# Keys and values per chunk and half of the heads, the next graph projected over four groups, tails without a lock, statistics two rows per step, longer gaps after residual transfers, denominators one step later

## The chip, the cores and the metric

The kernel runs on one NeuronCore of one Trainium2 chip. The metric is the device time of that core in microseconds (us). Every time below is a median of several executions. Each ratio compares a kernel with the kernel before, run on the same chip in the same rounds.

## The reference

One graph transformer layer over 8 graphs of 2048 nodes and 256 channels in fp32, all with one adjacency matrix. There are 8 heads of 32 channels.

```python
qkv = x @ w_qkv                                   # split in q, k, v, 8 heads of 32
scores = q @ k^T / sqrt(32), -1e9 where adj == 0
t = softmax(scores) @ v
x1 = layernorm(x + t) ;  f = relu(x1 @ w1 + b1) @ w2 + b2
out = layernorm(x + layernorm(x1 + f))            # x: the layer's input
```

## The kernel before

The work is a list of 1024 **items**: graph `f`, chunk of 512 queries `qc` (0 to 3), half of the heads `g` (0, 1) and block of 128 keys `mb` (0 to 15). Sixteen items with the same `f, qc, g` are a **group**. A step of the loop issues the scores of item t+2 and the values of item t, and slips in one or two **fillers**: pieces of projections, of denominators, of the tail of a chunk (attention output, norms, feed-forward, output). An **eviction** is the DVE instruction that adds the mask to scores in PSUM and writes them to a buffer p; two make one item, and ACT then takes the exp in place. A p buffer comes free when its values matmuls are done and its sum, on POOL or by a **chained add** (a transfer that accumulates one p into another), has been taken. A **residual** is the transfer that adds the layer's input x to a tail's rows; **statistics** are the means and variances of a norm. A **lump** is a step in which the loop must finish several projection banks at once.

```python
pp = tile_pool(name="pp", bufs=9)     # p: exp of the scores, 128 x 2048 fp32, 1 MB
ap = tile_pool(name="ap", bufs=1)     # acc: ONE accumulator of the same size
POOLED = (0, 1, 4, 7, 9, 12, 14)      # items whose p is summed on POOL into acc
CHAINS = ((2, 5, 8, 11), (3, 6, 10, 13))   # items summed by accumulating DMA
SUM = 4

def add_up(item):
    f, qc, g, mb = item
    grp = (f, qc, g)
    for chain in CHAINS:
        if mb in chain[1:]:           # "chained add"
            nc.gpsimd.dma_start(PT[f, qc, g, chain[0]], PT.pop(item), accum_op=ALU.add)
    if mb == POOLED[1]:
        ACC[grp] = ap.tile([P, 4, CH], F32, name="acc")
        nc.gpsimd.tensor_tensor(ACC[grp], PT.pop((f, qc, g, POOLED[0])), PT.pop(item), ALU.add)
    elif mb in POOLED[2:]:
        nc.gpsimd.tensor_tensor(ACC[grp], ACC[grp], PT.pop(item), ALU.add)

def denominator(f, qc, g):            # started SUM steps after the group's last item
    terms = [PT.pop((f, qc, g, LAST))] + [PT.pop((f, qc, g, chain[0])) for chain in CHAINS] + [ACC.pop(grp)]
    ps = bank()                       # while items run, there is ONE spare PSUM bank
    # ... 32 matmuls of ones with the terms into ps, a copy dT by ACT
    yield 1
    # ... 4 transposes of dT into bank(), read by DVE: rc = 1 / den
    if g == 1: start(items.index((f, qc, g, LAST)) + SUM + 2, tail(f, qc), urgent=True)

def norm(t):                          # three times per tail
    for j in range(TPC):              # TPC = 4 rows
        nc.vector.bn_stats(st, t[:, j, :]); nc.vector.bn_aggr(mv[:, j, :], st)
    yield 1                           # ... then POOL and ACT scale the rows

def tail(f, qc):
    while state["y"]: yield 0         # the lock: one tail at a time
    state["y"] = True
    # ... y = attention output / denominator (PE transposes, DVE)
    nc.gpsimd.dma_start(y, xin, accum_op=ALU.add)      # residual
    yield 4
    yield from norm(y)
    # ... feed-forward in fillers yT, w1, w2; second norm
    nc.gpsimd.dma_start(z, xin, accum_op=ALU.add)      # second residual
    yield 5
    yield from norm(z)
    nc.sync.dma_start(out[...], z)
    state["y"] = False

# in the loop, step t:
if mb:
    advance(t)                        # one filler
    if mb % 2: advance(t)             # in odd steps a second one
scores(items[t + LEAD]); values(items[t]); add_up(items[t])
```

PE's order is the program's order.

## Time and profile before

| kernel before | |
|---|---|
| time, median of 4 runs | 4099.34 us (4098.45 to 4102.65) |
| busy: PE, DVE, ACT, POOL | 81%, 67%, 60%, 64% |
| p buffers | 9, of 1 MB each |

The prediction below shows the main rows of the profile. A list of waits gives engine, tile and line, what it waited for: us in total, times, longest. The first view is the list of waits (engine, tile and line, what it waited for: us in total, times, longest), the second the page's rows for the first feed-forward matmuls and for the transfers of p (count, size, median us from issue to landing).

```profile
POOL acc L215 <- PE x L248: 147.0, 12, 16.7
...
DVE rc L259 <- PE x L254: 69.0, 8, 9.3
...
DVE p L181 <- DMA p<-p: 19.2, 9, 4.4
```

```profile
L300 PE MATMUL x<-turned,w1s 128*128 128x512 f32 x256 | 128.8, 626 | 3.3 <-ACT turned L292 1.0
...
p<-p POOLq DMA_DIRECT2D x384, 1024.0 KB, 9.3
```

By the list, POOL's first sum of a group waits for the old denominator 12 times of 64; the evictions on DVE hardly ever wait for a chained add to give back a p buffer (19 us), and the w1 matmuls find their PSUM bank free (3.3 us idle). The first of these is misleading: a wait for several things is put down to the one that came last by the profile. Set beside the denominators in the trace, the first sum starts within 0.4 us after their last matmul in all 63 groups that have an old denominator, both tiles that it adds having long been ready.

A measure is worked out from the trace: PE's **idle stretches** of over 0.3 us between the first and the last scores, summed by what the instruction that ended them waited for. For "behind an eviction", the wait is followed one step further, to what held DVE.

### The profile page before, as it was taken

The page shows a single profiled execution, that of the slowest core. Times are in us where ns is not written, and L with a number is a line of the kernel's source. Part 1 is how long each engine was busy: PE and PEld are TensorE (multiplying, and loading weights), DVE is VectorE, ACT ScalarE, POOL GpSimd, SP SyncE. Part 2 cuts the span into 40 slices and gives each one's busy share as a digit, 9 for nine tenths or more (in the row PEclk, how much of TensorE's full clock was granted, in tenths as well). Part 3 has the DMA queues.
Part 4 walks back from the last instruction along what each step waited for, and adds up shares of the span by engine and source line. Part 5 has one row for each costly group of instructions (what it writes and reads, how often), then busy time and mean ns, then how long its engine had stood idle before and what let it go on. Part 6 is the DMA issues. An engine that isn't in the chain of part 4 may idle for free. (4 is left out here: it accounts for less than half of the span.)

```text
span 4091.3 us, 52692 instructions
## 1 busy us (share of the span) xinstructions
PE 3308.0 (81%) x21508; PEld 1011.5 (25%) x21508; DVE 2745.5 (67%) x3175; ACT 2443.2 (60%) x1953; POOL 2624.4 (64%) x1355
## 2 busy tenths in 40 slices
PE   7777788878887888888878878877888878888883
PEld 3222132212222222222222222222222222222221
DVE  3777756777567774777647776477755777567772
ACT  4565555666566664666647666466655666556662
POOL 1576655776567774777747776477754777557774
PEclk9899899999999999999999999999999999999996
DMA  4766745666556664567746667376654677546663
GB/s 122 160 139 150 175 97 105 137 134 147 109 108 144 144 138 99 109 134 152 153 94 130 127 132 150 83 150 145 131 115 99 136 148 157 110 101 135 134 130 74
DMA packets 138792, 525.52 MB, mean 128 GB/s; under 512 B 10160, under 2 KB 76848, under 8 KB 85296
## 3 DMA queue, kind: packets, MB, share of 16 engines
q0 software_dynamic: 89088, 436.24, 53.4%
q1 hardware_dynamic: 49456, 85.86, 6.6%
q8 instruction: 170, 2.79, 0.3%
q14 instruction: 78, 0.64, 0.0%
HBM read 98.44 MB, written 20.97 MB: 29 GB/s over the span
## 5 line engine op out<-in xcount | busy, mean ns | idle before, releaser
L181 DVE TENSOR_TENSOR p<-s,mask 128x1024 f32<-128x1024 f32 x2048 | 2410.5, 1219 | 968.3 <-PE s L178 827.2
L183 ACT ACTIVATE p<-p 128x2048 f32<-128x2048 f32 x1024 | 1951.4, 1910 | 1326.1 <-DVE p L181 1135.6
L217 POOL TENSOR_TENSOR acc<-acc,p 128x2048 f32<-128x2048 f32 x320 | 1505.2, 4704 | 201.5 <-ACT p L183 196.8
L178 PE MATMUL s<-qT,kT 32*128 32x512 f32 x8192 | 1230.3, 671 | 472.9 <-DVE p L181 472.9
L195 PE MATMUL x<-p,v 128*32 128x512 f32 x8192 | 1140.1, 630 | 28.7 <-ACT p L183 28.4
L215 POOL TENSOR_TENSOR acc<-p 128x2048 f32<-128x2048 f32 x64 | 290.9, 4546 | 655.0 <-ACT p L183 508.0
L178 PEld LDWEIGHTS s<-qT,kT 32*128 32x128 f32 x8192 | 333.8, 191 | 1175.7 <-DVE p L181 1077.8
L212 POOL DMA_DIRECT2D p<-p x384 | 362.9, 977 | 362.9 <-ACT p L183 166.3
L195 PEld LDWEIGHTS x<-p,v 128*32 128x32 f32 x8192 | 163.9, 110 | 857.3 <-issue 480.1
L146 PE MATMUL x<-turned,wqkv 128*128 128x512 f32 x480 | 249.2, 645 | 50.9 <-ACT kT L148 29.0
L224 DVE BATCH_NORM_STATS2 st<-y 128x6 f32<-128x256 f32 x384 | 153.9, 401 | 144.3 <-DMA y<-in_x_dram 144.3
L235 ACT ACTIVATE y<-y,nb,rs 128x256 f32<-128x256 f32 x384 | 198.3, 588 | 62.1 <-POOL nb L232 62.1
L248 PE MATMUL x<-p,ones 128*32 128x512 f32 x1536 | 183.1, 610 | 15.8 <-ACT qT L148 14.8
L146 PEld LDWEIGHTS x<-turned,wqkv 128*128 128x128 f32 x480 | 85.4, 197 | 221.1 <-issue 79.8
L158 PE MATMUL x<-wqkv,turned 128*128 128x256 f32 x448 | 112.9, 395 | 31.1 <-ACT v L160 10.1
L300 PE MATMUL x<-turned,w1s 128*128 128x512 f32 x256 | 128.8, 626 | 3.3 <-ACT turned L292 1.0
L309 PE MATMUL x<-w2s,hT 128*128 128x256 f32 x512 | 127.6, 392 | 3.9 <-ACT hT L301 1.3
L228 POOL TENSOR_SCALAR rs<-mv 128x4 f32<-128x4 f32 x96 | 18.4, 191 | 147.9 <-DVE mv L225 144.2
L309 PEld LDWEIGHTS x<-w2s,hT 128*128 128x128 f32 x512 | 92.0, 189 | 69.1 <-ACT hT L301 31.1
L229 POOL TENSOR_TENSOR rs<-rs,mhalf 128x4 f32<-128x4 f32 x96 | 99.5, 1036 | 8.0
L158 PEld LDWEIGHTS x<-wqkv,turned 128*128 128x128 f32 x448 | 81.6, 192 | 77.3 <-ACT qT L148 28.5
L291 PE MATMUL x<-ident,y 128*128 128x128 f32 x256 | 44.6, 294 | 66.9 <-ACT turned L292 46.4
(70 smaller groups left out, 1550.0 us busy)
## 6 DMA issues: line engine op xcount, KB each, us to landing
p<-p POOLq DMA_DIRECT2D x384, 1024.0 KB, 9.3
y<-in_x_dram POOLq DMA_DIRECT2D x64, 512.0 KB, 7.2
mask<-md SPq DMA_DIRECT2D x28, 1024.0 KB, 15.4
in<-in_x_dram SPq DMA_DIRECT2D x32, 512.0 KB, 21.7
in<-in_adj_dram SPq DMA_DIRECT2D x32, 512.0 KB, 5.9
out_dram<-y SPq DMA_DIRECT2D x32, 512.0 KB, 8.3
md<-mask SPq DMA_DIRECT2D x4, 1024.0 KB, 12.7
wqkv<-in_L_gnn_w_qkv_dram SPq DMA_DIRECT2D x1, 768.0 KB, 4.6
```

Source lines behind the costliest of these rows:

```text
L146: nc.tensor.matmul(ps, wqkv[:, a, k0 + g * P:k0 + (g + 1) * P], xT[:, a, :], start=(a == 0), stop=(a == 1))
L158: nc.tensor.matmul(ps[:, (j - jj) * C:(j - jj + 1) * C], xT[:, a, j * P:(j + 1) * P], wqkv[:, a, 2 * C:], start=(a == 0), stop=(a == 1))
L178: nc.tensor.matmul(ps2[half][:, j, :], KT[f, mb // TPC][r:r + D, g, (mb % TPC) * P:(mb % TPC + 1) * P], QT[f, qc][r:r + D, g, :], start=Tr ...
L181: nc.vector.tensor_tensor(pt[:, 2 * half:2 * half + 2, :], ps, MK[f, qc][:, mb, None, :].to_broadcast([P, 2, CH]), ALU.add)
L183: nc.scalar.activation(pt, pt, AF.Exp, scale=1.0 / math.sqrt(D))
L195: nc.tensor.matmul(O[grp][r:r + D, :], V[f, mb // TPC][:, mb % TPC, g * P + r:g * P + r + D], PT[item][:, h, :], start=(mb == 0), stop=(mb ...
L212: nc.gpsimd.dma_start(PT[f, qc, g, chain[0]], PT.pop(item), accum_op=ALU.add)
L215: nc.gpsimd.tensor_tensor(ACC[grp], PT.pop((f, qc, g, POOLED[0])), PT.pop(item), ALU.add)
L217: nc.gpsimd.tensor_tensor(ACC[grp], ACC[grp], PT.pop(item), ALU.add)
L235: nc.scalar.activation(t[:, j, :], t[:, j, :], AF.Identity, bias=nb[:, j:j + 1], scale=rs[:, j:j + 1])
L248: nc.tensor.matmul(ps[r:r + D, :], cst["ones"], term[:, h, :], start=(n == 0), stop=(n == 3))
L309: nc.tensor.matmul(ps[:, (j - jj) * C:(j - jj + 1) * C], hT[:, d, j * P:(j + 1) * P], w2s[:, d, :], start=(d == 0), stop=(d == 1))
```

## The change

Intent: free K and V buffers half by half, so that the next graph's projections can be spread over four groups instead of running in lumps; let tails overlap, so that residual transfers no longer stand beside output and mask transfers; halve the DVE work that statistics put in one step. The denominators come one step later.

```diff
-    kp = ... bufs=NCK + 1          # and vp
+    kp = ... bufs=2 * NCK + 2      # tiles of half the heads; and vp
     # project(f, c): K and V written per half g; V by 16 matmuls of 128 columns per half
-            store[f, c] = dst
+                    KT[f, c, g] = pool.tile([P, CH], F32, name=name)
+        for g in range(2):
+            V[f, c, g] = vp.tile([P, TPC, P], F32, name="v")
-    SUM = 4
+    SUM = 5
     # norm
-        yield 1
+            if j % 2:
+                yield 1
     # tail
-        while state["y"]:
-            yield 0
-        state["y"] = True
         nc.gpsimd.dma_start(y, xin, accum_op=ALU.add)
-        yield 4
+        yield 5
         nc.gpsimd.dma_start(z, xin, accum_op=ALU.add)
-        yield 5
+        yield 7
         nc.sync.dma_start(out[...], z)
-        state["y"] = False
     # loop
+    AHEAD = [(NCK - 2, 1, 0), (NCK - 1, 0, MB // 2), (NCK - 1, 1, 0), (NCK - 1, 1, MB // 2)]
-            # projections of the next graph: chunk 0 at (3, 0, 0), chunks 1 to 3 at (3, 1, 4), (3, 1, 8), (3, 1, 12)
+        if f + 1 < F and (qc, g, mb) in AHEAD:
+            start(t, project(f + 1, AHEAD.index((qc, g, mb))))
-            while (nf, nmb // TPC) not in V:
+            while (nf, nmb // TPC, 1) not in V:
     # parameter loads: nc.sync.dma_start -> nc.scalar.dma_start
```

More of the change, by code (lines that the diff above doesn't have):

```diff
@@ L60, in fast_path @@
     ld = ctx.enter_context(tc.tile_pool(name="ld", bufs=3))
-    kp = ctx.enter_context(tc.tile_pool(name="kp", bufs=NCK + 1))
+    kp = ctx.enter_context(tc.tile_pool(name="kp", bufs=2 * NCK + 2))
     qp = ctx.enter_context(tc.tile_pool(name="qp", bufs=NCK + 1))
-    vp = ctx.enter_context(tc.tile_pool(name="vp", bufs=NCK + 1))
+    vp = ctx.enter_context(tc.tile_pool(name="vp", bufs=2 * NCK + 2))
     pp = ctx.enter_context(tc.tile_pool(name="pp", bufs=9))
@@ L76, in fast_path @@
     ident, identb, wqkv, w1s, w2s = cst["ident"], cst["identb"], cst["wqkv"], cst["w1s"], cst["w2s"]
-    state = {"pair": 0, "side": None, "turn": 0, "turned": False, "y": False}
+    state = {"pair": 0, "side": None, "turn": 0, "turned": False}
     def score_pair():
@@ L141, in project @@
         for store, pool, name, k0 in ((KT, kp, "kT", C), (QT, qp, "qT", 0)):
-            dst = pool.tile([P, 2, CH], F32, name=name)
+            if store is QT:
+                QT[f, c] = pool.tile([P, 2, CH], F32, name=name)
             for g in range(2):
+                if store is KT:
+                    KT[f, c, g] = pool.tile([P, CH], F32, name=name)
                 ps = bank()
@@ L147, in project @@
                                      start=(a == 0), stop=(a == 1))
-                nc.scalar.copy(dst[:, g, :], ps)
-                if g == 0:
-                    yield 1
-            store[f, c] = dst
-            yield 1
-        dst = vp.tile([P, TPC, C], F32, name="v")
-        for jj in range(0, TPC, 2):
+                nc.scalar.copy(KT[f, c, g] if store is KT else QT[f, c][:, g, :], ps)
+                yield 1
+        for g in range(2):
+            V[f, c, g] = vp.tile([P, TPC, P], F32, name="v")
             ps = bank()
-            for j in range(jj, jj + 2):
+            for j in range(TPC):
                 for a in range(2):
-                    nc.tensor.matmul(ps[:, (j - jj) * C:(j - jj + 1) * C], xT[:, a, j * P:(j + 1) * P],
-                                     wqkv[:, a, 2 * C:], start=(a == 0), stop=(a == 1))
-            nc.scalar.copy(dst[:, jj:jj + 2, :], ps.rearrange("p (b c) -> p b c", c=C))
-            if jj == 0:
+                    nc.tensor.matmul(ps[:, j * P:(j + 1) * P], xT[:, a, j * P:(j + 1) * P],
+                                     wqkv[:, a, 2 * C + g * P:2 * C + (g + 1) * P], start=(a == 0), stop=(a == 1))
+            nc.scalar.copy(V[f, c, g], ps.rearrange("p (j c) -> p j c", c=P))
+            if g == 0:
                 yield 1
-        V[f, c] = dst
         state["turned"] = False
@@ L177, in scores @@
                 r = D * (2 * half + j)
-                nc.tensor.matmul(ps2[half][:, j, :], KT[f, mb // TPC][r:r + D, g, (mb % TPC) * P:(mb % TPC + 1) * P],
+                nc.tensor.matmul(ps2[half][:, j, :], KT[f, mb // TPC, g][r:r + D, (mb % TPC) * P:(mb % TPC + 1) * P],
                                  QT[f, qc][r:r + D, g, :], start=True, stop=True)
@@ L194, in values @@
             r = D * h
-            nc.tensor.matmul(O[grp][r:r + D, :], V[f, mb // TPC][:, mb % TPC, g * P + r:g * P + r + D], PT[item][:, h, :],
+            nc.tensor.matmul(O[grp][r:r + D, :], V[f, mb // TPC, g][:, mb % TPC, r:r + D], PT[item][:, h, :],
                              start=(mb == 0), stop=(mb == LAST))
@@ L225, in norm @@
             nc.vector.bn_aggr(mv[:, j, :], st)
-        yield 1
+            if j % 2:
+                yield 1
         rs = small.tile([P, TPC], F32, name="rs")
@@ L343, in mask_ahead @@
             yield from turn_mask(qc, mc)
-    def projections(f, c0, c1):
-        for c in range(c0, c1):
-            yield from project(f, c)
     items = [(f, qc, g, mb) for f in range(F) for qc in range(NCK) for g in range(2) for mb in range(MB)]
     LEAD = 2
+    AHEAD = [(NCK - 2, 1, 0), (NCK - 1, 0, MB // 2), (NCK - 1, 1, 0), (NCK - 1, 1, MB // 2)]
     for c in range(NCK):
@@ L365, in fast_path @@
             load_mask(f + (qc + 1) // NCK, (qc + 1) % NCK)
-        if f + 1 < F and qc == NCK - 1:
-            if g == 0 and mb == 0:
-                start(t, projections(f + 1, 0, 1))
-            if g == 1 and mb % TPC == 0 and mb:
-                start(t, projections(f + 1, mb // TPC, mb // TPC + 1))
+        if f + 1 < F and (qc, g, mb) in AHEAD:
+            start(t, project(f + 1, AHEAD.index((qc, g, mb))))
         if mb:
@@ L375, in fast_path @@
         if t + LEAD < len(items):
-            nf, _, _, nmb = items[t + LEAD]
+            nf, _, ng, nmb = items[t + LEAD]
             t0 = t
-            while (nf, nmb // TPC) not in V:
+            while (nf, nmb // TPC, 1) not in V:
                 advance(t0)
@@ L540, in weight @@
         t = cst[name] = const.tile([P, 2, src.shape[1]], F32, name=name)
-        nc.sync.dma_start(t, src.rearrange("(a p) k -> p a k", p=P))
+        nc.scalar.dma_start(t, src.rearrange("(a p) k -> p a k", p=P))
     def row_of(pool, name, v):
         t = cst[name] = pool.tile([P, C], F32, name=name)
-        nc.sync.dma_start(t, bass.AP(tensor=v.tensor, offset=v.offset, ap=[[0, P], [1, C]]))
+        nc.scalar.dma_start(t, bass.AP(tensor=v.tensor, offset=v.offset, ap=[[0, P], [1, C]]))
     def cols_of(name, v):
         t = cst[name] = const.tile([P, 2], F32, name=name)
-        nc.sync.dma_start(t, v.rearrange("(a p) -> p a", p=P))
+        nc.scalar.dma_start(t, v.rearrange("(a p) -> p a", p=P))
     weight("wqkv", w_qkv)
```

## The prediction

> **What bounds the kernel now.** I read the cost groups of the page first, then busy time in windows of one group of 16 items, then the timeline where a window was long. The kernel is 1024 items (8 graphs, 4 query chunks, 2 head groups, 16 key blocks): eight score matmul records, two DVE evictions that add the mask, one exp on ACT, eight value matmul records. Projections, denominators and chunk tails are slipped between items as filler.
>
> ```profile
> L181 DVE TENSOR_TENSOR p<-s,mask 128x1024 f32<-128x1024 f32 x2048 | 2410.5, 1219 | 968.3 <-PE s L178 827.2
> L183 ACT ACTIVATE p<-p 128x2048 f32<-128x2048 f32 x1024 | 1951.4, 1910 | 1326.1 <-DVE p L181 1135.6
> L217 POOL TENSOR_TENSOR acc<-acc,p 128x2048 f32<-128x2048 f32 x320 | 1505.2, 4704 | 201.5 <-ACT p L183 196.8
> L178 PE MATMUL s<-qT,kT 32*128 32x512 f32 x8192 | 1230.3, 671 | 472.9 <-DVE p L181 472.9
> ...
> L224 DVE BATCH_NORM_STATS2 st<-y 128x6 f32<-128x256 f32 x384 | 153.9, 401 | 144.3 <-DMA y<-in_x_dram 144.3
> ```
>
> PE waits 473 us for DVE, DVE waits 827 us for PE: a loop. Two evictions take about 2.36 us; on the timeline a step without filler lasts 2.56 us (median of 509) and is held by DVE; a step with a 2 us filler lasts 4.05 us and is held by PE. No engine is full, so the question is which groups exceed the sum of their steps. Windows of graph 4, columns PE, PEld, DVE, ACT, POOL busy, PE clock, DMA share, GB/s:
>
> ```profile
> 2051.70:2146.80 95.10, 74.92 (x412) 27.19 (x412) 43.43 (x53) 44.81 (x44) 41.37 (x24) 0.98 0.42 89
> ...
> 2201.70:2246.90 45.20, 38.26 (x296) 9.78 (x300) 39.59 (x44) 33.12 (x23) 36.73 (x19) 1.00 0.64 139
> 2246.90:2313.10 66.20, 51.26 (x332) 14.79 (x330) 44.46 (x55) 37.87 (x30) 45.75 (x24) 0.90 0.69 140
> ```
>
> The first is the start of a graph, where projections run in a lump with DVE idle; the second is nearly ideal; in the third PE idles 15 us and DVE 22. The timeline of such a loss, and the view of the residual transfer's source line:
>
> ```profile
> 1853.05 0.38 SPq L319 DMA_DIRECT2D out_dram<-y  x1
> ...
> 1853.53 1.32 SPq L122 DMA_DIRECT2D mask<-md  x1
> ...
> 1856.31 1.61 POOL L281 DMA_DIRECT2D y<-in_x_dram  x1
> ...
> 1873.50 0.43 DVE L224 BATCH_NORM_STATS2 st<-y 128x6 f32<-128x256 f32 x1 [5.68 <-DMA y<-in_x_dram]
> ...
> 1876.94 2.09 PE L178 MATMUL s<-qT,kT 32*128 32x512 f32 x8 [8.05 <-DVE p L181]
> ```
>
> ```profile
>   DVE st L224: 124.0, 23
> ...
> DMA to landing us min/median/max: 7.0/16.9/20.4
> ```
>
> A tail may not start before the previous one has issued its output, so output, the next 1 MB mask and this residual start within 3 us of each other. The residual needs 16.9 us instead of 7.0, the statistics in DVE's queue wait for it, evictions wait behind them, PE starves for 8 us and then runs the next scores at half speed (2.09 instead of 1.14 us).
>
> **What the Trainium skill says.** "TensorE: Matmul & The Clock Gate", section "Architectural detail", calls the queues of ACT and DVE strict FIFOs: the trace agrees, ready evictions stood 5.68 us behind waiting statistics. The same page, "HAM oscillation", puts the idle time that throttles PE above about 3.4 us; here slow score or value matmuls followed 30 of 51 gaps of 2.1 to 2.4 us and nearly none of the shorter ones, so the measurement decides. Same page, "LDWEIGHTS": a load takes columns/1.2 GHz, 107 ns for 128. The trace agrees: two loads of one fp32 pair start 0.106 to 0.108 us apart, and identity transposes of 128 columns follow each other every 0.109 us although each load is recorded as 0.142 us. "Trainium Kernel Development and Optimization", "Key Constraints": queues of different engines share 16 DMA engines and save issue time only; that bears on the parameter loads moved to ACT.
>
> **The change part by part** (steps counted in the built order of both programs; the chip has not run it).
> 1. *V per half of the heads.* 8 records of 256 columns, 0.216 us apart (1.73 us), become 16 of 128 columns. By the transposes these should follow each other every 0.109 us: 1.74 us. Cost about 0. If the longer fp32 load (0.190 us) set the pace, 16 x 0.08 = 1.3 us for each of 64 banks, 80 us; I give that 15%.
> 2. *K and V in halves, projection spread.* K buffers of a half come free earlier, so projection of the next graph starts in chunk 2. Lumped steps fall from 21 to 15. A lump of three K/Q banks and two V banks took 16.1 us, less 2.6 for the step: 13.5; spread, five banks cost five times about 1.5 (4.05 - 2.56) = 7.5. At six later graph boundaries the three lumps (20.9 + 16.1 + 16.1) become two: two transposes with two V banks (estimate 14 us) and one of 16.1. The start window loses about 17 us, and 7 come back in chunks 2 and 3: -10 per boundary, -60.
> 3. *The lock on tails goes, residual gap 4 to 5 steps.* The residual is now issued some three steps (8 us) before output and mask, and its statistics come six steps after the last y eviction, about 15 us, against 7.0 us for an undisturbed landing. DVE waited 124 us for these residuals, 7 of it in the drain. I take 100 us as gone.
> 4. *Statistics two rows per step.* Four rows take 4 x 0.53 = 2.1 us of DVE at once, and PE then idles 2.28 us, just past the throttling limit:
>
> ```profile
> 1922.49 1.14 PE L178 MATMUL s<-qT,kT 32*128 32x512 f32 x8 [2.28 <-DVE p L181]
> ...
> 1923.56 1.93 PE L195 MATMUL x<-p,v 128*32 128x512 f32 x8
> ```
>
> DVE's work is unchanged, and where DVE sets the step it is not hidden. But each idle stretch should fall to about 0.4 + 1.1 = 1.5 us, at which PE stayed fast. Score and value groups ran 105 us too slowly in all; I count 55 us of the span, with part 3.
> 5. *Denominators one step later (4 to 5).* Matmuls unchanged. The POOL accumulation of the next group needs the single accumulator, free only after the denominator; it starts 2.6 us later, and with it the chained adds by DMA (median 9.3 us each) and the release of p buffers. In the second group of a chunk two POOL multiplies (5.3 us) now also stand before the first chained add. Counting down the chain, the buffer for item 12 comes free about when its eviction needs it. I charge 1.5 us in some 25 groups: +35.
> 6. *Start and drain.* x was issued at 7.35 us behind eleven parameter loads and now goes first: -5. In the drain the last tail no longer waits for the statistics of the one before: -8. The gap of the second residual (5 to 7) hits a wait of 20 us that lies mostly in the drain: 0.
>
> Sum: -60 - 100 - 55 + 35 - 13 = -193, and 0 for part 1. As a cross-check by windows of graph 4, in order: 95, 55, 45, 66, 46, 67, 51, 67 (493 us) should become about 78, 55, 48, 56, 49, 61, 50, 66 (463), so -30 for six graphs, -14 for graph 1, -20 for graph 0 and -13 for the ends: -227. I settle between, 215 below 4100: **3885 us**.
>
> **Rivals.** (a) The wait moves: p buffers held longer by POOL and by chained adds stall evictions. For it: POOL has 45.8 of 66 us busy in the long windows, which are to shrink to 56; transfers are 64% to 70% busy; one p buffer of slack goes. Against: POOL idles some 10 us per group before its first accumulation. It would cost up to 100 us more: 3985. (b) The 128-column V matmuls are bound by weight loads: +80 us on PE in steps that PE holds, about 3960. (c) The residual was hidden anyway and DVE's own work is the bound: then only the lumps and the ends pay, about 4010. Against it: PE ran at half clock right after those waits, and they are the largest gaps outside the lumps. (d) Better: waits and half-clock stretches all vanish, about 3820.
>
> **Range and chances.** Faster by 2% means below 4018 us, which needs less than half of the sum. Even (a), (b) or (c) alone stays just below; two together would not. I set 3815 to 3970, and 0.92 faster, 0.07 same, 0.01 slower.
>
> **What would show it.** Right: DVE's wait for the residual falls from 124 us to under 25, its landing to a median of 7 to 11 us; no PE gap above 5 us in graphs 1 to 7 outside lumps; the clock of the long windows returns from 0.90 to 0.97 or more; the start window shrinks from 95 to about 78 us; V banks stay near 2.0 us. Wrong: V banks of 2.5 us or more; evictions waiting over 60 us for POOL or chained adds; the residual still colliding with the mask load; windows of 45 us growing past 52.

## More of the kernel before

Of the 8 PSUM banks six hold scores, one the values of the running group, and one is the spare bank of all fillers.

Below, the V, K and AHEAD lines with the parameter loads are the **projection part**; SUM, the lock, the gaps and the statistics are the **tail part**.

## The result, and the profile after

The changed kernel is correct and takes **4218.69 us** (4215.43 to 4220.44, 4 runs). Its ratio to before is **1.029**, 95% interval 1.027 to 1.031: slower by 119 us, where 215 us of gain were predicted. Ratios here and below are the mean time of one kernel's runs over that of the other's of the same rounds, so not quite the ratio of the medians quoted.

The page's rows of the changed kernel that answer to those of before:

```profile
L180 DVE TENSOR_TENSOR p<-s,mask 128x1024 f32<-128x1024 f32 x2048 | 2409.2, 1218 | 1217.6 <-PE s L177 898.2
...
L214 POOL TENSOR_TENSOR acc<-p 128x2048 f32<-128x2048 f32 x64 | 290.7, 4543 | 911.0 <-PE x L248 570.9
...
L223 DVE BATCH_NORM_STATS2 st<-y 128x6 f32<-128x256 f32 x384 | 155.5, 405 | 42.8 <-DMA y<-in_x_dram 42.8
L297 PE MATMUL x<-turned,w1s 128*128 128x512 f32 x256 | 128.3, 624 | 39.6 <-DVE RS L261 21.5
...
p<-p POOLq DMA_DIRECT2D x384, 1024.0 KB, 10.5
```

The statistics' wait for residuals fell from 144.3 to 42.8 us, as forecast. But POOL's first sum now waits 571 us for the denominators' matmuls (147 before), DVE's idle time before evictions is 249 us longer, and the w1 matmuls wait 40 us, mostly for DVE's read of the denominators. The list of waits of the changed kernel shows what is new on DVE:

```profile
POOL acc L214 <- PE x L248: 570.9, 34, 25.6
...
DVE p L180 <- DMA p<-p: 189.0, 79, 5.8
```

Evictions, the instructions that set the loop's pace, wait for a chained add 79 times instead of 9. One such group on the changed kernel's timeline (start, duration, engine, line, idle time before it and what ended it):

```profile
3302.02 2.76 PE L248 MATMUL x<-p,ones 128*32 128x512 f32 x24
...
3305.83 4.54 POOL L214 TENSOR_TENSOR acc<-p 128x2048 f32<-128x2048 f32 x1 [4.61 <-ACT p L182]
...
3310.45 4.56 POOL L216 TENSOR_TENSOR acc<-acc,p 128x2048 f32<-128x2048 f32 x1
...
3314.95 1.78 POOL L211 DMA_DIRECT2D p<-p  x2
...
3322.24 1.14 PE L177 MATMUL s<-qT,kT 32*128 32x512 f32 x8 [1.19 <-DVE p L180]
...
3328.48 2.35 DVE L180 TENSOR_TENSOR p<-s,mask 128x1024 f32<-128x1024 f32 x2 [1.80 <-DMA p<-p]
...
3336.36 2.35 DVE L180 TENSOR_TENSOR p<-s,mask 128x1024 f32<-128x1024 f32 x2 [1.89 <-DMA p<-p]
3336.78 0.93 POOL L211 DMA_DIRECT2D p<-p  x1 [5.08 <-DMA p<-p]
...
3337.64 1.14 PE L177 MATMUL s<-qT,kT 32*128 32x512 f32 x8 [3.19 <-DVE p L180]
...
3338.71 1.94 PE L194 MATMUL x<-p,v 128*32 128x512 f32 x8
```

This group's first exp began at 3290.8. (The wait of the line at 3305.83 is put to an exp that ended 0.06 us after the denominators.) POOL cannot start its first sum before the old denominator has read the accumulator, at 3305.6: 15 us into the group. Two sums of 4.5 us follow, and only then, 24 us into the group, come the first chained adds. Evictions want p buffers back some 12 us later and stand still from 3326.7 and from 3334.5 for 1.8 and 1.9 us; PE idles 3.19 us and runs the next values at half speed (1.94 instead of 1.07 us). The wait after two rows of statistics, by contrast, is the short one that was predicted: 1.19 us at 3322.24, and PE stays fast.

Windows of graph 4 (columns: window, length, busy us of PE, PEld, DVE, ACT, POOL with instructions, PE clock, DMA share, GB/s), the first three the counterparts of those in the prediction, the last the final group of the graph:

```profile
2149.40:2228.60 79.20, 62.82 (x412) 22.83 (x408) 43.21 (x53) 44.82 (x44) 43.11 (x28) 1.00 0.51 106
2283.90:2334.90 51.00, 39.77 (x300) 9.86 (x293) 42.68 (x53) 35.23 (x27) 38.60 (x20) 0.97 0.67 126
2334.90:2396.00 61.10, 49.84 (x332) 14.32 (x324) 41.56 (x46) 37.79 (x30) 41.92 (x25) 0.97 0.60 135
...
2574.00:2652.40 78.40, 64.38 (x388) 22.59 (x384) 41.20 (x45) 40.75 (x35) 44.23 (x21) 0.96 0.59 133
```

The start of the graph shrank from 95 to 79 us and the long group from 66 to 61, at a clock of 0.97 instead of 0.90. The short group, 45 us before, became 51, and the last group grew from 66.8 to 78. All groups, as means of graphs 2 to 6, and whole graphs, in us (a group's window runs from its first exp to the next group's first):

| (qc, g) | 0,0 | 0,1 | 1,0 | 1,1 | 2,0 | 2,1 | 3,0 | 3,1 | sum | graph 0 | graph 1 | graph 7 |
|---|---|---|---|---|---|---|---|---|---|---|---|---|
| before | 96 | 55 | 45 | 66 | 46 | 67 | 52 | 66 | 494 | 496 | 496 | 480 |
| predicted (graph 4) | 78 | 55 | 48 | 56 | 49 | 61 | 50 | 66 | 463 | 476 | 482 | |
| changed | 80 | 55 | 51 | 61 | 52 | 69 | 57 | 77 | 504 | 529 | 540 | 480 |

And PE's idle stretches by cause, in us:

| PE idle | before | changed |
|---|---|---|
| behind evictions that stood behind statistics (with their wait for residuals) | 276 | 123 |
| behind evictions that waited for a chained add | 18 | **202** |
| fillers that waited for DVE to free the spare bank | 22 | **73** |
| fillers that waited for ACT | 181 | 196 |
| behind evictions that stood behind the adjacency's loads or their conversion (graph 0) | 26 | 58 |
| all | 698 | 802 |

Measured from the first exp of each group, POOL's first sum starts 20.4 us into it (mean; 16.3 before) and the first chained add is issued at 31.5 us (26.8 before).

So the expected gain was made (153 us behind statistics) and given back, with more, in waits that hardly existed before.

### The profile page after: what moved, and what is told of

It reads as the page before. It is cut to its first block, busy times and chain, and to the rows that moved or that the text cites. A ratio compares the mean times of both kernels' runs of the same rounds, so it can differ in the third digit from the quotient of the medians. Undisturbed runs are those within 1.5% of the kernel's fastest.

```text
span 4213.6 us, 53657 instructions
## 1 busy us (share of the span) xinstructions
PE 3327.3 (79%) x22020; PEld 1042.3 (25%) x22020; DVE 2738.3 (65%) x3175; ACT 2449.5 (58%) x1953; POOL 2627.2 (62%) x1355
## 5 line engine op out<-in xcount | busy, mean ns | idle before, releaser
L216 POOL TENSOR_TENSOR acc<-acc,p 128x2048 f32<-128x2048 f32 x320 | 1535.6, 4799 | 189.3 <-ACT p L182 176.6
L223 DVE BATCH_NORM_STATS2 st<-y 128x6 f32<-128x256 f32 x384 | 155.5, 405 | 42.8 <-DMA y<-in_x_dram 42.8
L158 PE MATMUL x<-wqkv,turned 128*128 128x128 f32 x896 | 119.8, 289 | 42.7 <-DVE y L274 14.4
L158 PEld LDWEIGHTS x<-wqkv,turned 128*128 128x128 f32 x896 | 109.0, 199 | 77.4 <-ACT v L160 19.7
L106 DVE TENSOR_SCALAR in<-in 128x1024 bf16<-128x1024 int32 x32 | 49.5, 1546 | 82.1 <-DMA in<-in_adj_dram 55.8
L311 POOL TENSOR_TENSOR y<-y,g2r 128x1024 f32<-128x1024 f32 x32 | 79.6, 2488 | 33.7 <-ACT y L235 33.7
## 6 DMA issues: line engine op xcount, KB each, us to landing
p<-p POOLq DMA_DIRECT2D x384, 1024.0 KB, 10.5
in<-in_x_dram SPq DMA_DIRECT2D x32, 512.0 KB, 24.2
```

What stands on the lines that cost most here:

```text
L158: nc.tensor.matmul(ps[:, j * P:(j + 1) * P], xT[:, a, j * P:(j + 1) * P], wqkv[:, a, 2 * C + g * P:2 * C + (g + 1) * P], start=(a == 0), s ...
```

## The experiments

Short names in the texts: **T1**, the loss comes from the chained adds and p buffers, held up by POOL behind the late denominator and its one accumulator (T1b: held up by their place behind the sums in POOL's queue); **T2**, the loss comes from two fillers in one step that share the one spare bank; **R1**, tails that overlap put POOL multiplies and transfers ahead of the chained adds, wherever the denominator stands; **R2**, the transfers themselves became slower. Kernels named a_ start from the changed kernel, b_ from the kernel before. All 17 gave correct results.

### Denominators one step earlier or later: a_sum4f and b_sum5f

```diff
+    SUM0 = 5      # graph 0 keeps its delay: with 4 there, the mask of the next chunk is read too early
-    SUM = 5       # b_sum5f is the mirror image: SUM0 = 4, SUM = 5
+    SUM = 4       # graphs 1 to 7
```

> The changed kernel with denominators back to four steps after a group for graphs 1 to 7 (five only for graph 0, where four would let an unfinished mask be read). Theory T1 (the late denominator holds the single accumulator, so POOL starts a group's sums late, the chained adds by DMA land late, and evictions wait for p buffers): DVE's wait for chained adds falls from 189 us to under 70, time 4060 to 4130 us. Rival R1 (the overlapping tails put POOL multiplies and transfers ahead of the chained adds, whatever the denominator's step): the wait stays above 140 us, time 4180 to 4215.

> The kernel before with denominators five steps after a group for graphs 1 to 7, nothing else. T1: DVE's wait for chained adds rises from 19 us to over 80, time 4150 to 4220 us. R1: the wait stays under 50 us, time 4095 to 4125.

Measured: a_sum4f 4204.06 us, ratio 1.026 (1.024 to 1.027); b_sum5f 4295.18 us, ratio 1.048 (1.047 to 1.050). In b_sum5f the evictions' wait for chained adds rose from 19 to 129 us and groups (0,1) and (3,0) from 55 and 52 to 62 and 59. So the one step costs 198 us in the kernel before, where the prediction charged 35 us. Its first sums start at 19.3 us and its chained adds at 29.9 us into a group, against 16.3 and 26.8. But taking the step back gives only 15 us in the changed kernel: the first sum comes earlier again (17.5 us), the first chained add hardly (29.3 us, against 31.5), the evictions' wait falls just from 189 to 173 us, and fillers that wait for ACT take back 35 us. The delay is enough to cause the wait, but it is not its only source there: b_sum5f went beyond T1's range (4150 to 4220 us), and a_sum4f came out as R1 had it. The lists of waits, first a_sum4f, then b_sum5f:

```profile
DVE p L180 <- DMA p<-p: 173.0, 56, 7.0
...
DVE p L181 <- DMA p<-p: 129.2, 47, 5.4
```

A source such as R1 names is in the trace. Between a group's first sum and its first chained add POOL runs tail multiplies of 2.3 us in the mean in a_sum4f and 1.8 us in the changed kernel, against 0.2 us in the kernel before and in b_sum5f. And the 198 us of b_sum5f are not all waiting: in the profiled runs PE's idle stretches grew by 68 us, while PE's busy time for the same matmuls grew by 121 us (3308 to 3429), at a mean granted clock of 0.924 instead of 0.947. So the delay shows twice, as idle time and as a lower clock; how much of the clock is due to the waits for chained adds was not tested.

One more reading: b_sum5f keeps the lock, and yet its statistics wait 61 us for residuals instead of 144.

### Sums in place, so that no accumulator has to come free: a_inpl and b_inpl

```diff
-    pp = ctx.enter_context(tc.tile_pool(name="pp", bufs=9))
-    ap = ctx.enter_context(tc.tile_pool(name="ap", bufs=1))
+    pp = ctx.enter_context(tc.tile_pool(name="pp", bufs=10))
-            ACC[grp] = ap.tile([P, 4, CH], F32, name="acc")
-            nc.gpsimd.tensor_tensor(ACC[grp], PT.pop((f, qc, g, POOLED[0])), PT.pop(item), ALU.add)
+            ACC[grp] = PT.pop((f, qc, g, POOLED[0]))
+            nc.gpsimd.tensor_tensor(ACC[grp], ACC[grp], PT.pop(item), ALU.add)
```

POOL sums into the group's own first p tile; the accumulator's memory becomes a tenth p buffer. All arithmetic stays.

> The changed kernel with POOL's sums taken in place in the group's first p tile; the accumulator's 8 KB become a tenth p buffer. POOL need no longer wait for the previous denominator. T1: POOL's waits for the denominator matmuls (571 us) vanish, DVE's wait for chained adds falls under 40 us, time 3950 to 4070 us. R1: DVE's wait falls by less than half, time 4130 to 4200.

> The same in-place sums in the kernel before. T1: there the late start was hidden, DVE waited only 19 us for chained adds, so time stays within 4060 to 4105 us. R1 says the same; a gain of over 60 us would mean that POOL's late start already cost time before the change.

Measured: a_inpl 4076.06 us, ratio 0.994 (0.991 to 0.996); b_inpl 4044.81 us, ratio 0.987 (0.985 to 0.989). The same edit is worth 143 us to the changed kernel and 53 us to the kernel before. The list of waits of a_inpl no longer has POOL waiting for the denominator among its larger entries, and the evictions' wait is a third:

```profile
DVE p L179 <- DMA p<-p: 61.9, 22, 4.8
```

The same group as above on the timeline of a_inpl; its first exp began at 3184.3:

```profile
3194.23 5.13 POOL L213 TENSOR_TENSOR p<-p 128x2048 f32<-128x2048 f32 x1
3199.44 4.56 POOL L215 TENSOR_TENSOR p<-p 128x2048 f32<-128x2048 f32 x1
3203.93 0.89 POOL L210 DMA_DIRECT2D p<-p  x1
```

The first sum starts 9.9 us into the group instead of 15.0, the first chained add 19.6 instead of 24.2, and none of this group's evictions waits for one. As means of all groups: 6.5 us (20.4 in the changed kernel) and 22.8 us (31.5). PE's idle behind chained adds falls from 202 to 36 us. Groups (1,0) and (2,0) come back from 51 and 52 to 47.8 and 48.3 us, the 48 and 49 that were predicted. T1's forecast was just missed (under 40 us of waiting, 3950 to 4070 us), R1's by far (4130 to 4200). The edit changes two things together, the start of the sums and a tenth buffer, and the two were not separated: with the accumulator kept, a tenth p buffer does not fit. (The tenth is not simply one more: the group's first p tile now stays occupied until the denominator has read it.)

### The chained adds ahead of the sums in POOL's queue: a_late

```diff
-        if mb == POOLED[1]:
+        if mb == 6:          # sums of items 0, 1, 4 are issued after the chained adds of 5 and 6
             ACC[grp] = ap.tile([P, 4, CH], F32, name="acc")
-            nc.gpsimd.tensor_tensor(ACC[grp], PT.pop((f, qc, g, POOLED[0])), PT.pop(item), ALU.add)
-        elif mb in POOLED[2:]:
+            nc.gpsimd.tensor_tensor(ACC[grp], PT.pop((f, qc, g, 0)), PT.pop((f, qc, g, 1)), ALU.add)
+            nc.gpsimd.tensor_tensor(ACC[grp], ACC[grp], PT.pop((f, qc, g, 4)), ALU.add)
+        elif mb in POOLED[3:]:
```

> The changed kernel; POOL's sums of items 0, 1 and 4 of a group are issued only after the chained adds of items 5 and 6, the accumulator still single and the denominators still five steps late. Theory T1b (POOL executes in order, so the first sum, which waits for the old denominator to free the accumulator, and the sum after it hold back the chained adds behind them; p buffers come free late): DVE's wait for chained adds falls from 189 us to under 80, time 4060 to 4150 us. Rival R2 (chained adds are late because the transfers themselves are slower, 10.5 against 9.3 us, next to the moved residual, output and mask): the wait stays above 140 us, time 4185 to 4230.

Measured: 4249.11 us, ratio 1.037 (1.035 to 1.039). The chained adds land in 7.9 us (median; 10.5 in the changed kernel, 9.3 before), so the transfers themselves are faster than in either kernel, and yet the evictions wait 217 us for them. R2 falls as a cause, though the time lies above its range. T1b's forecast (under 80 us of waiting) fails too: the order in the queue alone is no remedy. The first chained add goes out at 20.8 us instead of 31.5, but the first sum starts only at 28.5 us, so that items 0, 1 and 4 keep their p buffers longer, and the third chained add, behind three sums of together 14 us, goes out at 43.5 us instead of 40.3. POOL's work piles up after its late start, in whichever order it is queued.

### Two fillers on one spare bank: a_split, a_inpl_split, b_inpl_split

Where a denominator's transposes and a w1, K/Q or yT filler fall in one step, the second can only write the spare bank when DVE has read the first. In the changed kernel's trace a step with the transposes and w1 takes 5.93 us (17 times) and with K/Q 5.93 us (12 times); separate steps take 2.65 and 3.98 us, that is 6.63 for two steps against 5.93 + 2.56 for the pair and a plain step, a loss of 1.86 us each, some 54 us for the 29. First attempt, the second filler after the next scores:

```diff
         if mb:
             advance(t)
-            if mb % 2:
-                advance(t)
         ...
             scores(items[t + LEAD])
+        if mb % 2:
+            advance(t)
         values(items[t])
```

> The changed kernel; in odd steps the second filler is issued after the next item's scores instead of right behind the first filler. Theory T2 (the change puts two fillers in one step far more often, and both use the one spare PSUM bank, so the second waits 1.3 us for DVE or ACT to empty it): PE's idle time before fillers falls from 278 us by 60 to 130, time 4100 to 4170 us. Rival: the time is set by the p buffers anyway, and stays within 4195 to 4225.

> Both remedies on the changed kernel: sums in place in the first p tile (4076 us alone) and fillers split by the scores. If T1b and T2 are separate losses they add: 3960 to 4030 us. If one hides the other: 4050 to 4080.

> Both remedies on the kernel before (4045 us with sums in place alone). Before has only some dozen steps with two fillers, so T2 expects little from the split here: 4010 to 4045 us. If it ends below the changed kernel with both, the change loses on its own grounds even without these two waits.

Measured: a_split 4362.18 us, ratio 1.065 (1.063 to 1.068); a_inpl_split 4228.66 us, 1.034 (1.031 to 1.037); b_inpl_split 4223.88 us, 1.032 (1.029 to 1.034). A failed remedy: PE's idle in fillers that wait for DVE falls from 73 to 20 us, but in fillers that wait for ACT it rises from 196 to 317 us. The copy of the second filler now stands behind the next exp of 1.9 us in ACT's queue. All three times are far above what was expected. The runs say nothing for or against T2.

### No second filler behind a denominator's transposes: a_inpl_solo, a_solo, b_inpl_solo

```diff
+        state["solo"] = True       # in denominator(), before the transposes of dT
         ps = bank()
 ...
         if mb:
+            state["solo"] = False
             advance(t)
-            if mb % 2:
+            if mb % 2 and not (f and state["solo"]):
                 advance(t)
```

> Changed kernel with sums in place (4076 us) and, in graphs 1 to 7, no second filler behind a denominator's transposes. It takes apart 34 steps in which the transposes and another filler share the spare PSUM bank and which last 5.9 us; 12 projection banks move into the lumps. T2 (such a pair costs some 1.7 us more than its parts): 34 x 1.7 less some 10 for the lumps, time 4010 to 4045 us. If pairs cost nothing, the lumps decide: 4075 to 4110.

> The changed kernel, but in graphs 1 to 7 no second filler is slipped in behind the transposes of a denominator; sums on POOL stay as they are. If two fillers on one spare bank cost PE time by themselves, the gain measured with in-place sums (73 us) is found here too: 4135 to 4165 us, with PE's idle behind fillers that wait for DVE halved to about 36. If the waits for chained adds absorb it, because they and not the filler set the end of a group, it stays above 4195 with DVE's wait for chained adds risen above the 189 us of the changed kernel.

> The kernel before with the same two edits as the fastest of the changed ones (sums in place; in graphs 1 to 7 no second filler behind a denominator's transposes). It answers what the change itself is worth once both collisions are taken away from both sides. The changed kernel with them takes 4003 us. If the prediction's parts (residuals, statistics, lumps) are right apart from the collisions that it missed, this kernel stays near its value with in-place sums alone, 4045 (its fillers waited only 22 us for DVE), so 4025 to 4065, and the change is worth 20 to 60 us there. If the change is worth nothing even then, this one comes to 3995 to 4010 as well. If it is worth the 215 us that were predicted, it would have to take over 4150, which no theory of mine expects.

Measured: **a_inpl_solo 4003.14 us**, ratio 0.976 (0.973 to 0.978), faster than both kernels. a_solo 4248.46 us, ratio 1.036 (1.034 to 1.039). b_inpl_solo 4052.32 us, ratio 0.989 (0.987 to 0.992).

With the sums in place the edit is worth 73 us: the idle behind DVE in fillers is halved from 73 to 36 us, that behind chained adds falls to 10, and all of PE's idle falls from 689 to 632 us. Alone it costs 30 us. The same halving is seen (73 to 36), but the waits of the list go elsewhere:

```profile
POOL acc L214 <- PE x L248: 759.9, 44, 25.6
...
DVE p L180 <- DMA p<-p: 184.0, 70, 6.0
DVE st L223 <- DMA y<-in_x_dram: 128.9, 21, 15.4
```

POOL waits even longer for denominators (760 instead of 571 us), evictions as long as ever (184), and the residuals are late again (129 instead of 43): a step saved on PE is no use while POOL's chain sets the end of a group. My expectation that the wait for chained adds would rise above 189 us was wrong in its detail; the time went to residuals and to a lower clock (0.930; 188 slow score or value groups cost 144 us, against 96 us in the changed kernel). The effects of the two causes are not additive; the first hides the second.

Two windows of graph 4 in a_inpl_solo, the short and the long group:

```profile
2186.60:2235.10 48.50, 39.46 (x304) 9.82 (x300) 42.85 (x54) 35.22 (x27) 39.09 (x21) 1.00 0.67 128
2235.10:2294.70 59.60, 49.69 (x332) 14.39 (x324) 42.15 (x47) 37.83 (x31) 43.73 (x23) 0.97 0.68 149
```

The kernel before gains nothing from the edit beyond the sums in place (4045 and 4052 us): its fillers waited only 22 us for DVE. So with both collisions removed on both sides, the change is worth 4052 - 4003 = 49 us, or 1.2%.

### The tail part alone, and the lock alone: b_tail_sum5, b_tail_sum5_inpl, b_nolock

```diff
     # b_tail_sum5: SUM, lock, statistics and gaps as in the change; projections as before
     # b_tail_sum5_inpl: the same with the sums in place
     # b_nolock: the kernel before, without these lines
-        while state["y"]:
-            yield 0
-        state["y"] = True
-        state["y"] = False
```

> The kernel before with all of the change's tail parts (no lock on tails, statistics two rows per step, residual gaps 5 and 7, denominators 5 steps late) and none of its projection part (keys and values stay whole, projections of the next graph stay lumped, parameters stay on SP). If the projection part is about neutral on the chip, as the unchanged sum of lumped and spread windows suggests, this takes about the time of the changed kernel: 4190 to 4250 us. If the projection part is worth the 60 us that the prediction gave it, it takes 4265 to 4300. If the projection part is itself what costs the time (its lumps and three-bank steps at the end of chunk 2), it takes under 4150.

> The tail parts of the change on the projections of before (4324 us), now with the sums in place. If the cost of the tail parts is the wait of POOL's sums for the accumulator and the p buffers behind it, DVE's wait for chained adds falls from 181 us to under 70 and the time to 4130 to 4190. If the cost is elsewhere (collisions of tail fillers with lumps, ACT copies behind exps), it falls by less than 70, to over 4255.

> Kernel before without the lock on tails, nothing else. If the lock alone made residual, output and mask collide, DVE's wait for residuals falls from 124 us to under 60 and, by the same chained-add chain that T1b names, DVE's wait for chained adds rises above 60 us; time 4050 to 4130 us. If the longer gaps are what helps, the residual wait stays above 100 us and the time within 4085 to 4110.

Measured: b_tail_sum5 4323.51 us, ratio 1.053 (1.049 to 1.057); b_tail_sum5_inpl 4186.51 us, 1.021 (1.019 to 1.023); b_nolock 4430.15 us, 1.082 (1.078 to 1.086).

The tail part costs 224 us on the old projections. The projection part on top of it gains 105 us (4323.5 to 4218.7), and 110 us with the sums in place (4186.5 to 4076.1): more than the 60 us predicted. In the list of waits of b_tail_sum5 stand the same waits as in the changed kernel, and one that the changed kernel does not have:

```profile
POOL acc L215 <- PE x L249: 502.3, 33, 26.2
...
DVE p L181 <- DMA p<-p: 180.9, 76, 6.9
...
DVE rc L260 <- PE x L255: 98.6, 8, 16.8
```

The last is the start of a graph: the denominator, a step later, falls into one lump with three K/Q banks and two V banks, and group (0,0) takes 112 us against 96 before and 80 in the changed kernel. Sums in place take 137 us off (wait for chained adds 181 to 47 us), close to the 143 of a_inpl. What is left against b_inpl, 142 us, lies in 16 us of each of graphs 2 to 6 (18 us in group (0,0) alone), 29 us in graph 0, 13 in graph 1 and 19 in graph 7.

b_nolock was a miss: I expected a gain. Without the lock alone, PE's idle behind residuals and statistics stays at 262 us, that behind chained adds rises to 139, fillers wait 297 us for ACT (181 before), and evictions and statistics wait 159 and 206 us. These rises in idle make up most of the loss in the profiled runs: all of PE's idle stretches grow from 698 to 923 us, 121 us of it behind chained adds and 116 us in fillers that wait for ACT. The denominators still come after four steps here, so unlocked tails make the evictions wait by themselves; POOL's tail multiplies between first sum and first chained add are 1.9 us in the mean (0.2 before), and the first chained add is issued at 31.2 us (26.8 before):

```profile
DVE p L181 <- DMA p<-p: 158.7, 42, 6.1
```

So it was not the lock's removal that cut the residuals' wait: alone it raised the wait from 144 to 206 us, while the denominators' delay alone (b_sum5f) cut it to 61. Why fillers wait so much longer for ACT without the lock is open, and so is what each of the other tail parts is worth by itself: the changed kernel with the lock restored, the kernel before with two-row statistics alone and the projection part without the tail part all deadlock when built, and the tail part with SUM = 4 reads a mask too early. None of these four could be run.

### Statistics again four rows at once: a_inpl_norm4

```diff
             nc.vector.bn_aggr(mv[:, j, :], st)
-            if j % 2:
-                yield 1
+        yield 1
```

> Changed kernel with sums in place (4076 us) and four statistics rows at once as before the change. The prediction counted about 55 us for slow clocks after the 2.28 us idle stretches of four rows: then 4110 to 4140 us and over 60 more idle stretches of 2 to 2.5 us. Rival: DVE sets those steps either way and splitting saves little: 4065 to 4095 us.

Measured: 4199.92 us, ratio 1.024 (1.021 to 1.027), 124 us above a_inpl and 60 us above the upper end of what was expected. Splitting the statistics is worth more than twice the 55 us that I had counted. Slow score and value groups cost 134 us instead of 69, at a clock of 0.940 against 0.960: about half of the 124 us, and for the reason given. PE's idle time behind statistics is the same in both runs (149 and 150 us), only in 136 stretches instead of 74; shorter stretches, not less idle time, keep the clock up. The other half is mostly 43 us more PE idle elsewhere, of which chained adds take some 30.

### Output transfers on ACT's queue: a_outq, a_inpl_outq_solo

In graph 0 the adjacency's loads stand in SP's queue behind the output of a chunk; one stall there lasted 18.5 us in the changed kernel.

```diff
-        nc.sync.dma_start(out[...], z)
+        nc.scalar.dma_start(out[...], z)
```

> The changed kernel with the output transfers issued on ACT's queue, not SyncE's. Theory T3 (graph 0 got 33 us longer because adjacency loads stand in SyncE's queue behind an output that waits for a longer tail, then land 22 us late together with it): graph 0 falls from 529 us to under 505, DVE's wait for adjacency loads from 56 us to under 25, the rest within 20 us, time 4165 to 4200. Rival: the loads are late for want of a buffer (three, now shared with the earlier projection); graph 0 stays above 520, time 4200 to 4230.

> The fastest kernel so far (in-place sums on POOL, no second filler behind a denominator's transposes: 4003 us) with the output transfers issued from ACT's queue, so that no adjacency load stands behind an output in SP's queue. In the changed kernel that move gave 10 us, all in graph 0. If graph 0 still loses to it: 3990 to 3998. If that gain was hidden by other waits: within 4 us of 4003; if ACT's issue time delays exps: above 4010.

Measured: a_outq 4208.65 us, ratio 1.026 (1.024 to 1.029): 10 us, all of it in graph 0 (529 to 520 us). a_inpl_outq_solo **3985.96 us**, ratio 0.972 (0.970 to 0.974), the best version; 17 us better than a_inpl_solo, of which 5 are in graph 0. Most of the other 12 lie in graphs 4, 6 and 7, each 5 to 7 us shorter (graph 1 is 4 us longer); the cause was not looked into. Graph 0 still takes 24 us more than before, and b_tail_sum5 has the same graph 0 (531 us): the tail part makes it slower, not the projections or the parameter loads. Its cause is open.

## Why the prediction was wrong

**Right, or right in sign.** Step 1: V in 128-column matmuls costs nothing; a step with one V bank takes 4.05 us in both kernels where nothing else holds it, the bank's matmuls 2.05 us against 1.99. Step 2 in sign and place: the start of a graph takes 80 us, and the part as a whole is worth 105 to 110 us. Step 3's signs: the wait for residuals fell to 42.8 us (for the first residual of a tail from 124 to 4.8) and the landing of these from a median of 16.9 to 10.4 us; its cause, the lock, was wrong, as b_nolock and b_sum5f show. Step 4: idle after statistics is 1.2 us, and the step is worth 124 us. Nearly all signs listed as "Right" appeared, and of the signs listed as "Wrong" one did: evictions waiting over 60 us for chained adds (189). Step 6 was too large: in the profiled runs what lies before and after the eight graphs became 3 us shorter, not 13; x is issued 6.6 us earlier, but the first exp comes only 1.7 us earlier.

**The step that failed is 5, "Denominators one step later (4 to 5)": "I charge 1.5 us in some 25 groups: +35."** The mechanism in it was the true one: the single accumulator, late chained adds, late p buffers. The size was wrong. PE's idle behind chained adds rose by 184 us, and the delay alone costs 198 us in the kernel before, where waits of this kind came with a lower clock that the charge of 1.5 us a group leaves out. The delay is not the whole of it: with it taken back the evictions still wait 173 us (a_sum4f), and without any delay the lock's removal makes them wait 159 us (b_nolock). Step 3 booked the removal as pure gain; step 5 named the tail's multiplies on POOL before the first chained add (they stand there in 24 groups), but let the same 35 us cover them. I had counted down the chain with undisturbed durations and found that the buffer for item 12 comes free "about when its eviction needs it". I let the sums start 2.6 us later; they started 4.1 us later, and the first chained add came 4.7 us later, with no slack left to take that up: 79 waits of evictions in 64 groups. Rival (a) had the mechanism too, and with its 100 us on top was still some 50 short. The argument against it, that POOL idles some 10 us per group before its first accumulation, was void: that idle time was itself the wait for the accumulator, already before the change, and could not be used. I had read the list of waits, which puts only 12 of those waits to the denominators. That the residuals' stalls of the kernel before also gave the chained adds time to land, so that gaining step 3 took away cover from step 5, is plausible, but argued and not shown.

**A missing term: two fillers on one spare bank.** The sum had no entry for it. It shows as 51 us more PE idle in fillers (22 to 73), and removing it is worth 73 us, once the sums are in place. The steps with two fillers could be counted in the built order before the run.

**Step 2's bookkeeping.** "The start window loses about 17 us, and 7 come back in chunks 2 and 3": the first half was right (16), but groups (2,1), (3,0) and (3,1) took back 2 + 5 + 11 = 18 us. (The terms shown for the three lumps make 53.1 - 30.1 = 23 us; the 17 fits only if the denominator's own step of 5.5 us, which ran in the first lump and now stands alone, is counted too, and the prediction doesn't say so.) With both collisions removed, (2,1) takes 60.8 us, as predicted (61), and (3,0) and (3,1) 54.8 and 69 instead of 50 and 66: part of this was collision, part real.

**Graphs 0 and 1** were to gain 20 and 14 us and lost 34 and 44. This is open, apart from the 10 us of the output's queue.

By graphs, the distance from the prediction's cross-check (227 us of gain) to the profiled runs (122 us longer) is 349 us: graphs 2 to 7 account for 228 (predicted six times -30, measured five times +9.7 and -0.4), graph 1 for 58, graph 0 for 54, and the ends for 10.

What stays of the change when the collisions are gone is 49 us. In the means of graphs 2 to 6, b_inpl_solo against a_inpl_solo: (0,0) 95.8 to 84.9, (1,1) 63.8 to 59.0 and (2,1) 65.5 to 60.8 gain; (1,0), (2,0), (3,0) and (3,1) lose 1 to 6 us each; graph 0 loses 18. So even with the missed terms priced, a gain of 215 us was too much: in-place sums alone already shorten the kernel before by 53 us.

## What to carry to other kernels

A buffer that is freed by a late consumer and wanted by an early producer is a chain of its own: count its slack in us before moving either end, and price zero slack as a wait in every round, not as a rounding error. When one part of a change removes a stall, ask which other chain had been hiding behind that stall. Before believing a small loss, test the parts in combination: here one step's delay of the denominators alone cost 198 us, the lock's removal alone 333, all tail parts together 224, and two small edits (sums in place, no second filler behind the transposes) turned a loss of 2.9% into a gain of 2.4%.

## What the Trainium skill lacked or had wrong

- "DMA: Bandwidth & Descriptors" says that accumulating transfers must be issued from GpSimd, but gives no time for one. Here 1 MB between two p tiles lands 6.8 us after issue at best, 9.3 us in the median before (longest 21.0), 10.5 in the changed kernel, and each issue holds POOL's queue for about 0.98 us, behind whatever sum runs there.
- "TensorE: Matmul & The Clock Gate", section "HAM oscillation", gives as its rule that idle gaps of PE above some 3.4 us are harmful. Here shorter ones were. In the kernel before the granted clock fell to half 73 times between the first and the last scores, 44 times with no idle stretch above 2.5 us in the 3.4 us before; of 66 stretches of 2.1 to 2.4 us 36 were followed by half clock, of 33 stretches of 1.2 to 1.5 us 2. Of the 138 score or value groups that ran slow (105 us), some 66 followed stretches of 1.5 to 2.5 us and most others stretches above 3.4 us.
- "GPSIMD Engine Reference", section "Performance versus the Vector engine", has 4497 ns for an fp32 add of 2048 elements per partition. That is the floor here (shortest 4492 ns), not the mean. In the changed kernel first sums of a group took 4.54 us and sums into the accumulator 4.80 us in the mean. Two such sums stand between a late accumulator and the first chained add.
